# Half of the last memory layer moved into attention, a PSUM piece of its own for the rotation, and TensorE products without a reader

## The chip, the core and the metric

The kernel runs on one core of a Trainium2 chip. It is one launch; the metric is the time of that launch on the device in microseconds (us). The core has TensorE (matrix products, "PE" in the profile; its weight loads are "PEld"), VectorE ("DVE"), ScalarE ("ACT"), GpSimd ("POOL") and SyncE ("SP", which issues most DMAs). Each takes its own instructions in the order in which they were put. Products are written to PSUM, which has 8 banks of 2 KB in each of 128 partitions; everything else lies in SBUF.

## What is computed

A two-block network on an input `x` of 2 sequences ("batches") of 512 tokens and 512 features, all in float32. Block 0 is a state space layer with a quantised feed-forward layer before and after it. Block 1 is attention with a memory layer before and after it. Only block 1 matters here:

- The memory layer normalises `x` to `h` (mean and variance of a token), and adds half of `h` to `x`. From `h` it forms `q = h Wq` (64 features) and `Wr q` (48). Routing scores against 128 slots pick the best 8 slots of a token; a softmax over these of `q`'s scores against the keys weighs the slots' values. A gate of the token multiplies the result before it is added to `x`. The gate is made of `log1p(var(h))`, divided by its mean over all tokens of both batches, and of a small network `gelu(h Wu1 + bu1) Wu2`.
- Attention normalises `x`, makes 32 query heads and 8 key and value heads of 16 features, rotates queries and keys by position, applies a causal softmax, and adds the output product to `x`.

## The kernel before

**Tokens and tiles.** `x` is held in SBUF as eight tiles `x[t]` of 128 tokens by 512; tiles 0 to 3 are batch 0 and 4 to 7 are batch 1. A norm (`norm_parts`) has the steps `stats(t)` (L168, L169), `root` (square root on ScalarE, L172), `over` (reciprocal), `centre(t)` (L179) and `turn(t)`: four transposes on TensorE into a PSUM tile (L201) and a copy on ScalarE to the transposed `hT[b]` (L205).

**The last stages** are `memory(0)`, `attention` and `memory(1)`, one after the other. Each has its own PSUM pools. A pool has a tag and a number of buffers; a buffer is as large as the largest tile of the tag, and a new tile in a buffer waits until everything that read the old one is done. In the memory layers there are the tags `tr`, `mm`, `dd` and `y`, with two banks each. In attention there are `pq` (two buffers of two banks), `mx` (two of one bank), `av` (one) and `s` (one). `ps` puts a tile with a tag that attention hasn't got into `s`.

**Order.** Inside `in_order` the instructions of each engine stay in the order of the code. Outside, the planner of the framework orders them, and two ordered parts may be interleaved by it. The parts of `memory` behind the norm are ordered by the planner; the norm of `memory(1)` (`norm_in_order`) and all of attention are in order.

**Attention's start** (`attend`, first loop). For batch 0 it goes over five weight tiles `u` (keys, then four of queries), spread over iterations `n`. `qk` makes the projection in two halves of two products (L1425), then `hi` on ScalarE and `lo` and `r` on VectorE (L1414, L1415, L1438), which all read the projection. `rotate` of the tile before multiplies `hi` and `lo` by a permutation (L1448), into the second half of the same PSUM tile `p` that holds this iteration's projection; VectorE and GpSimd finish the rotation (L1451, L1452). `rotated` splits it again (L1463, L1464) and `spread_out` writes queries and keys as their products need them (L1474 to L1481). Between them lie the transposes of the norm's batch 1 (`turn`), the value product (L1488), and the first `maxima`.

**Attention's tiles.** 2 batches times 8 tiles of four heads, with four steps `j` each (64 steps). In step `j`:

- `maxima` for the next tile: scores on TensorE into `mx` (L1507), row maxima on VectorE (L1517);
- `weights_of`: mask and score products into both `pq` buffers (L1540, L1553), then the exponentials on ScalarE (L1559);
- `weigh` of the step before: products with the values into `av` (L1569);
- at j=0 `normalise` of the tile before: transposes into `s` (L1582), reciprocal and product on VectorE (L1589, L1590);
- `jobs`: a table of further pieces for step (tile, j), run after the above;
- after j=3 `turn_maxima`: transposes into `s` (L1527) and a copy on VectorE (L1529).

The order within a step is written out by hand:

```python
order = {
    0: (units[0], "weigh", "weights", "normalise", units[1]),
    1: ("weights", units[2], "weigh", units[3]),
    2: ("weights", units[4], "weigh", units[5]),
    3: ("weights", "weigh"),
}
```

In tiles 0 to 9 the jobs are batch 1's `qk` (halves in j=1 and j=2 of even tiles), `rotate` (j=3), `rotated` and `spread_out` (next, odd tile), and its values. In tiles 9 to 12 they are the output product of batch 0, one token tile in each: `out_turn` at j=1 (L1601, copy L1605) and `out_product` at j=2 (L1613, added to `x` at L1615). In tiles 14 and 15 they are three quarters of batch 1's output product. Nearly all of these use `s`.

**`memory(1)`** takes both batches: norm, first product `pz` (L1125) with a gelu, `pq` (L1151), `prq` (L1158), scores `psc` (L1167, L1168) with the choice of slots on VectorE (L1176 to L1192), exponential (L1195), transposes `pw` (L1198), the gate, the slots' product `pmo` (L1239) and its addition to `x` (L1242). `store` then writes `x` out in eight DMAs.

Of the kernel before, what the change touches and what calls it, by code (L numbers as in the profile page):

```python
# [10 lines left out]
F32 = mybir.dt.float32  # L11
# [63 lines left out]
        return (g, b) if g < NG else None  # L75


class Kernel:
    def __init__(self, tc, ctx, a, out):
        self.tc, self.nc, self.a, self.out = tc, tc.nc, a, out  # L80
        nc = self.nc
        self.const = ctx.enter_context(tc.tile_pool(name="const", bufs=1))
        self.xpool = ctx.enter_context(tc.tile_pool(name="xpool", bufs=1))
        self.dram = ctx.enter_context(
            tc.tile_pool(name="scratch", bufs=1, space=bass.MemoryType.DRAM)
        )
        masks = self.const.tile([P, 4, P], F32, name="masks")
        nc.sync.dma_start(out=masks, in_=a["masks"])
        self.ident = masks[:, 0, :]
        self.upper = masks[:, 1, :]  # L90
        self.below = masks[:, 2, :]
        self.ones = masks[:, 3, :]
        self.eps = self.const.tile([P, 2], F32, name="eps")
        nc.vector.memset(self.eps[:, 0:1], EPS)
        nc.vector.memset(self.eps[:, 1:2], 4.0 * EPS)
        self.npool = ctx.enter_context(tc.tile_pool(name="npool", bufs=1))
        self.x = [
            self.xpool.tile([P, D], F32, name=f"x{t}", tag=f"x{t}") for t in range(NT)
        ]
        self.normed = None  # L100
        self.load(0)

    def load(self, b):
# [48 lines left out]
        return t  # L152


    def norm_parts(self, tag, each=None, gain=None):

        nc, pool = self.nc, self.npool
        mv = pool.tile([P, NT, 2], F32, tag="mv", name=f"mv_{tag}", bufs=2)
        rstd = pool.tile([P, NT], F32, tag="rstd", name=f"rstd_{tag}", bufs=2)
        hT = [  # L160
            self.xpool.tile([P, KD, S], F32, tag=f"hT{b}", name=f"hT{b}_{tag}")
            for b in range(NB)
        ]
        done = {}

        def stats(t):
            st = pool.tile([P, 6], F32, tag="bnst", name=f"bnst_{tag}{t}", bufs=3)
            nc.vector.bn_stats(out=st, in_=self.x[t])  # L168
            nc.vector.bn_aggr(out=mv[:, t, :], in_=st)  # L169

        def root(t, to):
            nc.scalar.activation(  # L172
                rstd[:, t:to], mv[:, t:to, 1], AF.Sqrt, bias=self.eps[:, 0:1]
            )

        def centre(t):
            r = rstd[:, t : t + 1]
            h = pool.tile([P, D], F32, tag="h", name=f"h_{tag}{t}", bufs=3)
            nc.vector.tensor_scalar(  # L179
                out=h, in0=self.x[t], scalar1=mv[:, t, 0:1], scalar2=r,  # L180
                op0=ALU.subtract, op1=ALU.mult,
            )
            done[t] = h if each is None else each(t, h)

        def start(t):
            stats(t)
            root(t, t + 1)
            r = rstd[:, t : t + 1]
            nc.vector.reciprocal(r, r)
            centre(t)  # L190

        def over(t, to):
            nc.vector.reciprocal(rstd[:, t:to], rstd[:, t:to])

        self.norm_steps = stats, root, over, centre

        def turn(t, bank="tr"):
            h = done.pop(t)
            pt = self.ps(bank, [P, KD, P], f"hps_{tag}{t}")
            for k in range(KD):  # L200
                nc.tensor.transpose(pt[:, k, :], h[:, k * P : (k + 1) * P], self.ident)  # L201
            c = t % NC
            dst = hT[t // NC][:, :, c * P : (c + 1) * P]
            if gain is None:
                nc.scalar.copy(dst, pt)  # L205
            else:
                nc.vector.tensor_tensor(
                    out=dst, in0=pt, in1=gain.unsqueeze(2).to_broadcast([P, KD, P]), op=ALU.mult
                )

        return hT, start, turn

    def norm(self, tag, each=None, gain=None):
        hT, start, turn = self.norm_parts(tag, each, gain)
        for t in range(NT):
            start(t)
            turn(t)
        return hT

    def norm_in_order(self, tag, each):  # L220

        with self.in_order():
            hT, _, turn = self.norm_parts(tag, each)
            stats, root, over, centre = self.norm_steps
            for b in range(NB):
                for t in range(b * NC, (b + 1) * NC):
                    stats(t)
                root(b * NC, (b + 1) * NC)
            for b in range(NB):
                over(b * NC, (b + 1) * NC)  # L230
                for t in range(b * NC, (b + 1) * NC):
                    centre(t)
                    turn(t)
        return hT


# [810 lines left out]


    def memory_setup(self, pool):
        nc, a = self.nc, self.a  # L1050
        m = self.m = {}
        for name, shape in (
            ("m_wq", [P, KD, BOT]), ("m_wr", [BOT, RDIM]), ("m_keys", [BOT, NSLOT]),
            ("m_vals", [P, KD, NSLOT]), ("m_wvd", [P, KD, VB]), ("m_wvu", [VB, D]),
            ("m_wu1", [P, KD, P]), ("m_cols", [P, 2]),
        ):
            m[name] = pool.tile(shape, F32, name=name)
            nc.sync.dma_start(out=m[name], in_=a[name])
        m["rel"] = pool.tile([P, NSLOT], F32, name="m_rel")
        nc.sync.dma_start(out=m["rel"], in_=a["m_rel"].partition_broadcast(P))  # L1060
# [11 lines left out]
        for k in range(KD):  # L1072
# [1 line left out]
                p[:VB, :NSLOT], lhsT=m["m_wvd"][:, k, :], rhs=m["m_vals"][:, k, :],  # L1074
                start=k == 0, stop=k == KD - 1,
            )
        vd = pool.tile([VB, NSLOT], F32, name="m_vd")
        nc.scalar.copy(vd, p[:VB, :NSLOT])
        p = self.ps("tr", [P, D], "p_vu")
        nc.tensor.matmul(p, lhsT=vd, rhs=m["m_wvu"], start=True, stop=True)  # L1080
# [3 lines left out]
    def memory(self, n, then=None):  # L1084
# [3 lines left out]
        with self.tc.tile_pool(name=f"mem{n}", bufs=1) as pool:  # L1088
# [8 lines left out]
                )  # L1097
                return h

            hT = (self.norm_in_order if n else self.norm)(f"m{n}", each)  # L1100


            lv = pool.tile([P, NT], F32, name=f"lv{n}")
# [128 lines left out]
            with self.in_order():  # L1232
# [3 lines left out]
                for t in range(NT):  # L1236
# [13 lines left out]
                        root(t + 1 - NC, t + 1)  # L1250
                    if t == NC:
                        over(0, NC)
                        for one in range(NC):
                            if one == NC - 1:
                                turn(0)
                            centre(one)
                        for one in range(1, NC):
                            turn(one)
                if then is not None:
                    over(NC, NT)  # L1260
                    for t in range(NC, NT - 1):
                        centre(t)
                    return hT, turn, centre

# [47 lines left out]
    def attend(self, turn, centre):  # L1314
# [7 lines left out]
        def measure(n=1):  # L1322
            for one in ahead[:n]:
                self.maxima(0, 0, *one)
            del ahead[:n]


        for n in range(len(first) + 2):
            if n > 1:
                self.rotated(*first[n - 2])  # L1330
            p = self.ps("pq", [P, 2, S], f"pqk_{n}") if n <= len(first) else None
            for half in range(2):
                if n < len(first):
                    self.qk(*first[n], half, p[:, 0, :])
                if n > 3:
                    measure()
                if n < NC and not half:
                    turn(NC + n, "mx")
            if n == 0:
                centre(NT - 1)  # L1340
            if n == 1:
                self.project_values(0)
            if 0 < n <= len(first):
                self.rotate(*first[n - 1], p[:, 1, :])
            if n > 1:
                b, u = first[n - 2]
                tags = ("mx", "mx", "av", "s") if u == 4 else ("av", "s")
                for i, tag in enumerate(tags):
                    self.spread_out(b, u, i, tag)
# [9 lines left out]
        for t, u in ((0, 4), (2, 0), (4, 1), (6, 2), (8, 3)):  # L1359
# [4 lines left out]
            for i in range(4 if u == 4 else 2):  # L1364
                n, j = divmod(4 * t + 5 + i, 4)
                job(n, j, self.spread_out, 1, u, i, "s")
        job(3, 3, self.project_values, 1)
        for c in range(NC):
            job(9 + c, 1, self.out_turn, 0, c, 0, KD)
            job(9 + c, 2, self.out_product, 0, c, 0, KD, "s")  # L1370
            for j, f, *tag in ((1, self.out_turn), (2, self.out_product, "mx")):
                n, j = divmod(4 * 14 + j + c, 4)
                job(n, j, f, 1, c, 0, KD - 1, *tag)
# [9 lines left out]
        for n, (b, t, j) in enumerate(steps):  # L1383
            to = tiles[n // NC + 1] if n // NC + 1 < len(tiles) else None
            for one in order[j]:
                if one == "weights":
                    self.weights_of(b, t, j)
                elif one == "weigh":
                    if n:
# [19 lines left out]
        self.nc.scalar.copy(oT, pt)  # L1409
        for c in range(NC):  # L1410
            self.out_product(1, c, k, KD, "mx", {k: oT[:, c, :]})

    def parts(self, hi, lo, x):
        self.nc.scalar.copy(hi, x)  # L1414
# [207 lines left out]
def body(tc, a, out):  # L1622
    with ExitStack() as ctx:
# [8 lines left out]
        with k.banks("psum_e", dd=2, y=2, tr=2, mm=2):  # L1632
# [1 line left out]
            ctx.enter_context(k.weights("b", 6, 4))  # L1634
            k.attention_setup(ctx.enter_context(tc.tile_pool(name="attn_const", bufs=1)))
            parts = k.memory(0, lambda: k.norm_parts("a"))
        with k.banks("psum_b", pq=2, mx=2, av=1, s=1):
            k.attention(*parts)
        with k.banks("psum_c", **four):
            k.memory(1)  # L1640
        k.store()


# [137 lines left out]
```

## Time and profile before

| what | us |
|---|---|
| median of three runs | 2813.09 |
| lowest and highest of them | 2789.83, 2822.13 |
| the profiled execution, time | 2795.29 |
| its span | 2793.5 |
| TensorE busy in it | 2689.8 (96%) |
| VectorE busy | 2030.9 (73%) |
| ScalarE busy | 1102.6 (39%) |
| first step of attention's tiles | 2454 |
| last output product of attention added to `x` | 2720.9 |
| last product of `memory(1)` added to `x` | 2790.5 |

Times in the trace are us from the start of the span. A group row names the line, the engine, the operation, its output and inputs, and the shape. Two numbers in front of a timeline row are start and length; a bracket at its end is the idle time of the engine before it and what ended it. In a list of waits, the three numbers are total us, number of times and longest. In a table of stretches, the clock is the share of full speed that TensorE was granted. Matmul records overlap their successors, so the distance of starts tells their cost better than their length.

### The profile page before, as it was taken

What the parts mean: (1) busy time and instruction counts of PE and PEld (TensorE: products, weight loads), DVE (VectorE), ACT (ScalarE), POOL (GpSimd) and SP (SyncE); (2) the same over time, 40 slices, a digit from 0 to 9 for tenths busy, and PEclk for the clock granted to TensorE, in tenths of its full rate; (3) what the DMA queues carried; (4) which work ended last, traced back from release to release, by engine and by line L of the source; (5) the groups of instructions that cost most, each with busy time, mean ns of one, the idle gap of its engine ahead of it and who ended that gap; (6) DMA issues with size and microseconds to landing.
All of it is one profiled execution on the core that took longest, in us unless ns stands there. A gap on an engine that the chain in (4) does not pass through costs nothing.

```text
span 2793.5 us, 33412 instructions
## 1 busy us (share of the span) xinstructions
PE 2689.8 (96%) x12208; PEld 1398.5 (50%) x12208; DVE 2030.9 (73%) x3632; ACT 1102.6 (39%) x2411; POOL 522.1 (19%) x344
## 2 busy tenths in 40 slices
PE   8999999999999999999999999999999999788887
PEld 4444555555555555555555555555554444444443
DVE  7836877877888788787888878878886533555545
ACT  2214443544444344344443444434443212244442
POOL 0001131313313123132321322313230000110000
PEclk9999999999999999999999999999999999889996
DMA  7623133223223322322322332232121020000000
GB/s 209 198 89 113 72 107 128 87 91 123 96 83 124 113 72 103 129 87 80 126 105 83 121 105 80 106 128 87 68 99 46 27 84 1 0 1 1 1 1 31
DMA packets 75621, 237.77 MB, mean 85 GB/s; under 512 B 9825, under 2 KB 10401, under 8 KB 58945
## 3 DMA queue, kind: packets, MB, share of 16 engines
q1 hardware_dynamic: 70416, 226.00, 23.2%
q10 hardware_dynamic: 4752, 8.65, 0.8%
q8 instruction: 97, 1.59, 0.2%
q0 software_dynamic: 288, 0.98, 0.1%
q14 instruction: 68, 0.55, 0.1%
HBM read 223.80 MB, written 11.80 MB: 84 GB/s over the span
## 4 chain that ended last, share of the span: by engine, by line
PE 85%; DVE 9%; ACT 4%; issue 1%; DMA 0%; ACTq 0%; SPq 0%; DVEq 0%
PE pg L715 15%; PE po L832 14%; PE cp_h L715 14%; PE fo L501 5%; PE fmm L334 5%; PE py L989 4%; PE st L908 3%; PE fy L334 2%; DVE acc_h L729 2%; PE py L998 2%; PE cp_BT L715 2%; PE cp_CT L715 2%; PE ht L1042 2%; PE w L1553 1%; PE pqk L1425 1%; PE fdd L334 1%
## 5 line engine op out<-in xcount | busy, mean ns | idle before, releaser
L715 PE MATMUL pg<-hT_s,wi 128*128 128x512 f32 x1024 | 472.5, 604 | 14.4 <-issue 6.9
L832 PE MATMUL po<-wo,yg 128*128 128x512 f32 x1024 | 460.7, 593 | 0.5 <-DVE yg L1009 0.5
L715 PE MATMUL cp_h<-hT_s,wi 128*128 128x512 f32 x1024 | 460.6, 592 | 0.0
L806 DVE TENSOR_TENSOR_SCAN M<-rows,later 128x512 f32<-128x512 f32 x256 | 457.8, 1827 | 0.0
L1016 POOL TENSOR_TENSOR ssum<-ssum,sq 128x512 f32<-128x512 f32 x112 | 142.2, 1270 | 1233.0 <-ACT sq L1015 1233.0
L715 PEld LDWEIGHTS pg<-hT_s,wi 128*128 128x128 f32 x1024 | 184.2, 189 | 221.6 <-issue 213.4
L729 DVE SCALAR_TENSOR_TENSOR acc_h<-cp_h,small,acc_h 128x511 f32<-128x511 f32 (+2 forms) x384 | 286.1, 745 | 9.0
L832 PEld LDWEIGHTS po<-wo,yg 128*128 128x128 f32 x1024 | 184.8, 190 | 184.4 <-issue 183.6
L715 PEld LDWEIGHTS cp_h<-hT_s,wi 128*128 128x128 f32 x1024 | 184.6, 190 | 183.6 <-issue 183.6
L822 POOL TENSOR_TENSOR Cs<-CT,rows 128x768 f32<-128x768 f32 x128 | 251.9, 1968 | 17.6 <-PE py L998 15.7
L918 DVE SCALAR_TENSOR_TENSOR st<-st,whole,st 128x64 f32<-128x64 f32 x512 | 108.8, 274 | 125.7 <-ACT st L913 125.7
L734 ACT ACTIVATE th_h<-acc_h 128x512 f32<-128x512 f32 x128 | 80.5, 629 | 292.2 <-DVE acc_h L729 286.5
L861 ACT ACTIVATE hd<-ht,end 128x64 f32<-128x64 f32 x768 | 170.4, 323 | 35.8 <-DVE hc L853 35.7
L1015 ACT ACTIVATE sq<-yg 128x512 f32<-128x512 f32 x112 | 70.6, 630 | 286.9 <-DVE yg L1009 286.9
L820 DVE TENSOR_TENSOR M<-M,CB 128x512 f32<-128x512 f32 x256 | 164.4, 683 | 0.1
L811 ACT ACTIVATE M<-M 128x512 f32<-128x512 f32 x128 | 80.7, 630 | 199.1 <-DVE M L806 199.1
L853 DVE TENSOR_TENSOR hc<-ht,dt 128x512 f32<-128x512 f32 x128 | 88.0, 688 | 86.2 <-PE ht L1042 86.2
L1517 DVE CUSTOM_DVE_ANT_0 j<-s,future 128x384 f32<-128x384 f32 (+3 forms) x256 | 112.8, 486 | 48.8 <-PE s L1507 48.6
L989 PEld LDWEIGHTS py<-M,hc 128*64 128x64 f32 x2048 | 109.4, 136 | 68.2 <-issue 64.7
L989 PE MATMUL py<-M,hc 128*64 128x128 f32 x2048 | 140.5, 279 | 1.1 <-DVE M L820 1.1
L908 PEld LDWEIGHTS st<-hd,Btok 128*128 128x128 f32 x768 | 104.0, 191 | 70.0 <-issue 42.4
L738 DVE SCALAR_TENSOR_TENSOR v<-v,pg 128x512 f32<-128x512 f32 x128 | 87.4, 683 | 49.8 <-ACT v L849 47.7
(325 smaller groups left out, 3776.6 us busy)
## 6 DMA issues: line engine op xcount, KB each, us to landing
rows<-rows SPq DMA_DIRECT2D x128, 1024.0 KB, 4.7
wi<-in_w_in_dram SPq DMA_DIRECT2D x144, 256.0 KB, 3.5
wo<-in_w_out_dram SPq DMA_DIRECT2D x64, 256.0 KB, 3.1
keep<-w ACTq DMA_DIRECT2D x33, 256.0 KB, 3.5
wk<-keep SPq DMA_DIRECT2D x33, 256.0 KB, 2.7
wi<-in_q_dram SPq DMA_DIRECT2D x44, 128.0 KB, 3.1
sc<-in_s_dram SPq DMA_DIRECT2D x44, 128.0 KB, 3.2
wi<-in_q_dram SPq DMA_DIRECT2D x11, 256.0 KB, 3.3
```

Of the source, the lines that this page charges most:

```text
L334: nc.tensor.matmul(dst, lhsT=w[:, k, :], rhs=x[:, k, :], start=start and k == 0, stop=stop and k == 1, skip_group_check=True,)
L501: nc.tensor.matmul(po, lhsT=act[ht][:, b, c * P : (c + 1) * P], rhs=w2[ht], start=ht == 0, stop=ht == NHT - 1,)
L715: self.nc.tensor.matmul(p, lhsT=wt[:, k, :], rhs=self.hT[b][:, k, :], start=k == 0, stop=k == KD - 1)
L729: self.nc.vector.scalar_tensor_tensor(out=acc[:, s:], in0=p[:, : S - s], scalar=w[:, 3 - s : 4 - s], in1=acc[:, s:], op0=ALU.mult, op1=ALU ...
L806: self.nc.vector.tensor_tensor_scan(out=m, data0=rows[:, i, 0, :], data1=self.later, initial=0.0, op0=ALU.add, op1=ALU.mult,)
L820: self.nc.vector.tensor_tensor(out=m, in0=m, in1=sh["CB"], op=ALU.mult)
L822: self.nc.gpsimd.tensor_tensor(out=cur.Cs, in0=sh["CT"][:, P:].unsqueeze(1).to_broadcast([P, 2, S - P]), in1=cur.rows[:, :, 1, P:], op=ALU ...
L832: self.nc.tensor.matmul(self.po[c], lhsT=p2.yg[:, c * P : (c + 1) * P], rhs=self.wo[p2.ct], start=p2.q == 0, stop=p2.q == PAIRS - 1,)
L861: nc.scalar.mul(hd[:, c, ch], p1.pt[:, c, ch], self.dec["dt_end"][:, b * NC + c, h0 + i : h0 + i + 1],)
L908: nc.tensor.matmul(pst[:, c, :], lhsT=self.sh[p1.g, p1.b]["Btok"][:, c, :], rhs=hd[:, c, :], start=True, stop=True,)
L989: nc.tensor.matmul(py[ch, cs], lhsT=hc[:, c, ch], rhs=p1.M[i].rearrange("p (c t) -> p c t", c=NC)[:, c, :], start=c == 0, stop=c == 0, ski ...
L1016: nc.gpsimd.tensor_tensor(out=self.ssum, in0=self.ssum, in1=sq, op=ALU.add)
```

## The change

It has four parts.

1. **Memory in parts.** A class `Memory` holds the last memory layer cut into steps for one batch or one token tile: `learn`, `gelu`, `query`, `route`, `learned`, `score`, `weight`, `gate`, `add`. Batch 0's steps up to `weight` become jobs in attention's tiles 11 to 15; its norm's statistics stand behind the output products, which are moved closer together (tiles 9 to 11). All of their PSUM tiles go to `s`, since attention has no `tr`, `dd`, `y` of its own. `end_last`, after attention, does batch 1 and the gates and additions of both batches. The variance of `h` is now worked out from that of `x` (`spread`), and the second `bn_stats` and `bn_aggr` of each tile are gone from this layer. `memory(0)` keeps the old code. `norm_in_order` is gone.
2. **The rotation's piece.** In attention's start the projection and the rotation get a PSUM tile each, of the same tag `pq`, and `turn` comes after the second half of `qk`.
3. **Products that nothing reads.** `keep_up(n)` puts `n` products of bfloat16 constants, 128x128 by 128x512, into a tile that has no reader: two after each of the six `maxima` in attention's start (`s`), one in front of `weights_of` in every step but j=2 (`s`, 48 in all), six in front of the transposes of the norm that leads to attention (`dd`), and eight, then two, in front of the transposes of the last norm (`y`).
4. **Pools.** Three constants of the memory layer and an intermediate one lie in a pool that is closed after their use, whose space goes to the next pools; the last memory layer's small tiles lie in a pool that is open through attention.

```diff
@@ class Memory (new; steps shortened)
+    def half(self, t, h):
+        x = self.k.x[t]
+        self.nc.vector.scalar_tensor_tensor(
+            out=x, in0=h, scalar=0.5, in1=x, op0=ALU.mult, op1=ALU.add
+        )
+        return h
...
+    def learn(self, b):
+        pz = self.k.ps("dd", [P, S], f"pmz{n}_{b}")
+        for k in range(KD):
+            nc.tensor.matmul(
+                pz, lhsT=m["m_wu1"][:, k, :], rhs=self.hT[b][:, k, :],
+                start=k == 0, stop=k == KD - 1,
+            )
+        z, th = self.work("acc", f"mz{n}_{b}"), self.work("th", f"mt{n}_{b}")
+        nc.scalar.activation(z, pz, AF.Identity, bias=m["m_cols"][:, 0:1])
...
+    def weight(self, b, c):
+        if c == 0:
+            self.wT[b] = self.work("wT", f"mw{n}_{b}")
+        pw = self.k.ps("dd", [P, P], f"pmw{n}_{b}_{c}")
+        nc.tensor.transpose(pw, self.at.pop(b * NC + c), self.k.ident)
+        nc.scalar.copy(self.wT[b][:, c * P : (c + 1) * P], pw)
@@ memory_setup
+        with self.tc.tile_pool(name="mem_made", bufs=1) as made:
+            self.memory_constants(pool, made)
...
+            at = made if name in ("m_vals", "m_wvd", "m_wvu") else pool
+            m[name] = at.tile(shape, F32, name=name)
@@ memory(0), before the norm that leads to attention
                         over(0, NC)
+                        self.keep_up(6, "dd")
@@ end_last (new)
+            for t in range(NC, NT):
+                stats(t)
+            root(NC, NT)
+            over(NC, NT)
+            for t in range(NC, NT):
+                centre(t)
+                self.keep_up(2 if t > NC else 8, "y")
+                m.turn(t)
+        m.spread()
+        m.learn(1)
+        m.gelu(1)
+        m.query(1)
+        m.route(1)
+        m.learned(1)
+        m.gate(0)
+        for c in range(NC):
+            m.score(1, c)
+            m.weight(1, c)
+        for t in range(NC):
+            m.add(t)
+        m.gate(1)
+        for t in range(NC, NT):
+            m.add(t)
@@ attend, start
                 self.maxima(0, 0, *one)
+                self.keep_up(2)
...
-            p = self.ps("pq", [P, 2, S], f"pqk_{n}") if n <= len(first) else None
+            p = self.ps("pq", [P, S], f"pqk_{n}") if n < len(first) else None
+            rot = self.ps("pq", [P, S], f"prot_{n}") if 0 < n <= len(first) else None
             for half in range(2):
                 if n < len(first):
-                    self.qk(*first[n], half, p[:, 0, :])
+                    self.qk(*first[n], half, p)
...
-                if n < NC and not half:
+                if n < NC and half:
                     turn(NC + n, "mx")
...
-                self.rotate(*first[n - 1], p[:, 1, :])
+                self.rotate(*first[n - 1], rot)
@@ attend, jobs: at(n, f) is step n of 64, tile n // 4, j = n % 4
         for c in range(NC):
-            job(9 + c, 1, self.out_turn, 0, c, 0, KD)
-            job(9 + c, 2, self.out_product, 0, c, 0, KD, "s")
+            at(37 + 2 * c, self.out_turn, 0, c, 0, KD)
+            at(38 + 2 * c, self.out_product, 0, c, 0, KD, "s")
+            at(38 + 2 * c, stats, c)
+            at(46 + c, centre, c)
+            at(47 + c, m.turn, c)
+            at(56 + 2 * c - (c == 3), m.score, 0, c)
+            at(57 + 2 * c - (c == 3), m.weight, 0, c)
+        at(45, root, 0, NC)
+        jobs[divmod(46, NC)].insert(0, (over, (0, NC)))
+        for n, f in ((51, m.learn), (52, m.query), (53, m.gelu), (54, m.route), (55, m.learned)):
+            at(n, f, 0)
@@ attend, steps
                 if one == "weights":
+                    if j != 2:
+                        self.keep_up(1)
                     self.weights_of(b, t, j)
@@ keep_up (new)
+    def keep_up(self, n, tag="s"):
+        p = self.ps(tag, [P, NC, P], f"up{self.ups}")
+        self.ups += 1
+        for _ in range(n):
+            self.nc.tensor.matmul(
+                p, lhsT=self.mask[:, 0, :],
+                rhs=self.mask[:, 1:2, :].to_broadcast([P, NC, P]), start=True, stop=True,
+            )
```

## The prediction

> **What bounds the kernel now.** I read first the page's slices (where TensorE, "PE", is not full), then busy time by stage, then the chain of waits of each stage, then the timeline of single steps.
>
> The page's slices, of 70 us each:
> ```profile
> PE   8999999999999999999999999999999999788887
> ...
> PEclk9999999999999999999999999999999999889996
> ```
> TensorE is full up to slice 34; only the last six, which are the memory layer, attention and the second memory layer, are not, and only there does its clock drop. The change touches these alone. Busy time by stage (length, then PE, PEld, DVE, ACT, POOL, clock, DMA share, GB/s):
> ```profile
> 2393.00:2460.00 67.00, 52.62 (x203) 30.16 (x205) 31.75 (x81) 20.70 (x35) 12.67 (x10) 0.81 0.00 1
> 2460.00:2660.00 200.00, 178.90 (x1629) 95.92 (x1628) 119.91 (x470) 87.20 (x138) 12.78 (x10) 1.00 0.01 1
> 2660.00:2716.00 56.00, 49.23 (x427) 26.01 (x427) 23.08 (x84) 22.91 (x38) 0.00 (x0) 0.97 0.00 1
> 2716.00:2794.00 78.00, 59.92 (x150) 26.62 (x149) 46.21 (x139) 20.46 (x42) 0.00 (x0) 0.71 0.07 27
> ```
> Attention's 16 tiles (2454 to 2716) run at 89% PE and full clock: work added there costs nearly its own length. The tail after 2716 is a latency chain at a clock of 0.71: work taken from there is cheap to take. What TensorE waited for, first within 2407 to 2454 (attention's start), then within 2454 to 2716 (us, times, longest):
> ```profile
> PE pqk L1448 <- DVE r L1438: 5.7, 3, 2.1
> ...
> PE w L1540 <- ACT w L1559: 11.2, 25, 0.7
> PE prot L1448 <- DVE r L1438: 4.1, 5, 0.8
> PE pm L1527 <- DVE r L1451: 3.9, 5, 0.8
> PE av L1569 <- ACT w L1559: 1.5, 1, 1.5
> ...
> PE pao L1613 <- ACT q L1477: 0.7, 1, 0.7
> ```
> The steady wait is for the exponentials (11.2). All `prot`, `pm` and `pao` rows are waits for the one-bank PSUM tag "s": its reader has to finish first. The fillers in the steps use that same tag. One even tile shows what this means:
> ```profile
> 2466.66 1.98 PE L1425 MATMUL pqk<-hT_a,a_wqk 128*128 128x512 f32 x4
> 2468.48 0.39 PE L1540 MATMUL w<-mask 128*128 128x128 bf16 x4
> ...
> 2470.73 0.47 PE L1448 MATMUL prot<-hi,spread 128*128 128x512 f32 x1 [0.81 <-DVE r L1438]
> ```
> The bank is not free until 2470.7, 2.3 us after the projection; today TensorE does 1.4 us of `weights_of` and `weigh` in that time.
>
> **The tail.** Last `x` at 2720.87, end 2793.5: 72.6 us for both halves. After it only batch 1 is left:
> - norm: statistics to 2722.5, root and reciprocal 0.7, then four times centre 0.55 and add 0.66 (the second statistics, 0.69 + 0.18 a tile, go) = 4.8, last transpose and copy 1.2: to 2729;
> - `learn` and `query`, 8 products at 0.86 = 6.9; q copy 0.58, `route` 1.0, rq copy 0.58: to 2738; gelu beside it. Ln (table load 1.28) is beside too;
> - four scores of 2.05 on DVE (8 instructions at 0.28) = 8.2, batch 0's four adds at 0.75 = 3, gates about 2: to 2751;
> - exponential, transpose, copy, gate 2; four adds 3 to 5; last store 3.0 as now: to 2760.
>
> Gain 33. With the clock at half throughout, 8 us more (25); with everything hidden, 37. `keep_up(8)` and its pairs lie where TensorE waited 6.4 for `h_m` in all: free.
>
> **Attention's start.** `rotate` shares a tile with the projection, so it waits for `r` of the next one: 5.7 in three waits. With its own piece it waits only for its inputs. The projection's pieces now follow each other in one slot, whose readers need 2.1 (hi 0.58, lo 0.69, r 0.68 and hand-overs); turn 0.43, rotate 0.7 and spread 0.9 cover 2.0 of that: gain about 5.5. The 12 fillers of `measure` cost at most 12 x 0.23 (the nearest row, a one-pass 128x512 product of L1474, starts each 0.23 at full clock) = 2.8, of which 1.3 falls into waits for `top`; and they bear on the half clock from 2440 to 2461, worth up to 3 to 4. `turn` behind the second half of `qk` moves a copy behind `hi`: 0. I take -7 (ends -3 and -9). `keep_up(6)` in front of `turn` lies in a 2.5 wait for `h_a`: 0, and up to -3 if the clock is back sooner; I take -1. The constants' pool that is closed early makes `a_wv` and the first weights wait for `p_vu` (2343.6): with them, on SP's queue, `rope`, `future` and `a_wo` behind. 3.6 MB take some 16 us at the 159 to 362 GB/s at which they came (2266 to 2288); first use is 2401: 0.
>
> **Fillers in the tiles.** 48, three a tile. Those of j=1 fall mostly into the 0.8 wait for the exponentials, once `normalise` has been read (bank free 1.6 after its start, before that wait ends): 0 in most tiles. Those of j=0 stand behind `turn_maxima`, whose reader the step needs anyway: 0.23. Those of j=3: 0.23 plus the bank. 32 x 0.23 = 7.4, with five visible ones of j=1 1.2. The bank's waits, behind which `weights_of`, and so ScalarE's exponentials and the next `weigh`, are queued:
> - even tiles 0 to 8, behind `qk`: 2.3 instead of 0.81, 1.4 x 5 = 7;
> - odd tiles to 7, behind `spread_out`: 0.7 (the `pao <- ACT q` row) x 4 = 2.8; tile 2 at j=1, where the copy queues behind the exponentials, 1.4;
> - tiles 9 and 10, j=3, behind `out_product`: product end to DVE's `x` read 0.95 x 2; tiles 12, 13 and 15 behind copies, 0.7 + 0.7 + 0.3: 3.6. Of j=1, tiles 10 to 14 have such a wait in place of the 0.8 for the exponentials: 1.5 over it.
>
> Sum 25. Its lower end is 8 (no wait beyond the fillers), its upper 33.
>
> Here a rule matters. The Trainium skill, "TensorE: Matmul & The Clock Gate", section "Part 1: The HAM clock gate", lets the clock fall only after an idle window of some 3.4 us. By it, waits of up to 2.3 cost no clock and fillers in the steps buy none. But the row of the one 1.5 wait says otherwise:
> ```profile
> 2664.00:2668.00 4.00, 2.54 (x22) 1.37 (x24) 2.11 (x7) 2.82 (x5) 0.00 (x0) 0.80 0.00 0
> 2668.00:2672.00 4.00, 3.37 (x30) 1.99 (x30) 1.76 (x5) 1.94 (x2) 0.00 (x0) 0.78 0.00 0
> ```
> 0.20 x 4 + 0.22 x 4 = 1.7 of clock lost, about 3.4 us at half. By the row each long wait may cost 1.5 more, by the rule 0. Since the 2.1 waits of 2424 to 2432 left the clock at 1.00, I take the rule for the forecast and the row for a rival.
>
> **Memory's first half in attention.** On PE: transposes 4 x 0.6, `learn` and `query` 6.9, `route` 0.9, `learned` 1.0, scores 4 x 0.72, weights 4 x 0.33: 15.3. All use "s", so: `turn_maxima` behind a copy in tiles 9 to 13, 4 x 0.68 + 0.4 = 3.1; jobs at j=0 behind `normalise`, 5 x 0.45 = 2.2; in tiles 14 and 15 `out_turn` behind scores and weights, 2.5. 23 together (ends 15 and 30). DVE gets 15 us over five tiles (scores 8.2, centres 4.8, gelu 2.5) at 58% busy: hidden, but `maxima` behind gelu waits 1. ACT's copies: 8 us at 43%, in the waits above. Statistics and root stand within attention already (`bnst_m` at 2663.3, root at 2664.3); an earlier root has its inputs sooner: the 1.5 wait for the exponentials and half its clock loss go, -2.5. Moved `out_turn` and `out_product` are the same work.
>
> Sum: 25 + 23 + 1 - 2.5 = 46 in the tiles, -33 in the tail, -8 at the start: +5. The profiled run took 2795.3 (span 2793.5), so 2800; the median of the three runs is 2813 (2790 to 2822), 18 above that run, so about 2817. I predict 2816. About 1% (28 us) is the least that these runs tell from no change.
>
> **Rivals.**
> - *Fillers hide* (0.22): the bank is free in time or ScalarE sets the pace anyway. Tiles 8 + 17 - 2.5, tail -36, start -9: -22, 2791. For it: 11.2 of waits for exponentials. Against: `prot` and `pao` rows show the bank's wait in the open.
> - *The clock falls in the steps* (0.20), the slower side: the waits for "s" let TensorE cool as the 1.5 wait did. Some 16 waits of over 0.7, at 1.5 each, +24: +29, 2842. It decides if the clock from 2454 to 2720 is under about 0.87. For it the two rows above; against it 2460 to 2660 at 1.00 with ten 0.8 waits.
> - *The tail doesn't shorten as it should* (0.13): the two batches overlap there today (batch 1's products lie between batch 0's scores), so that taking one away leaves batch 1's chain at half clock. Gain 20: +18, 2831.
> - *Forecast* (0.45): 2800 to 2830.
>
> **How the numbers follow.** Faster by over 1% needs the first rival nearly whole, with the prologue's best: 0.13. Slower by over 1% is half of the second, a fifth of the third and a little of the forecast's edge: 0.16. The rest is 0.71. The range, 2784 to 2842, runs from the first rival with the tail's best to the second, and takes in the runs' spread.
>
> **What would show it.** After: tail from last `x` to the end 37 to 42 with a clock above 0.8; `prot` without waits before its tiles and the first exponential 6 earlier; attention's tiles some 46 longer, with waits at the filler for `r` of L1438 (five of about 2.2), `q`, `x` and copies. Wrong if the filler's rows show no waits (then faster), if the clock in the tiles drops (slower), or if a scheduler outside the written order spreads the tail's products.

## The result and the profile after

| | before | after |
|---|---|---|
| median of 22 runs each, us | 2808.2 | 2822.3 |
| lowest to highest, us | 2788.8 to 2822.1 | 2809.2 to 2836.1 |
| profiled execution, time (span), us | 2795.3 (2793.5) | 2829.5 (2827.7) |

The ratio after to before is 1.0063, with a 95% interval of 1.0046 to 1.0080: 18 us slower by the ratio (the two medians lie 14 apart), within the 1% that was taken as "no change". The forecast was +5. The spans of the two profiled runs differ by 34.2: before's lies 13 below its median, after's 7 above. The stages below are therefore read for where time went, and the ratios for how much.

The page's slices of after, 71 us each:
```profile
PE   8999999999999999999999999999999998889887
...
PEclk9999999999999999999999999999999997998988
```
The last slices show a shorter tail at a higher clock than before, and the slices with attention's tiles (34 to 36) are no longer full, with a clock that drops to 0.7 in one of them. Stretches of after, with the same columns as before (length, PE, PEld, DVE, ACT, POOL, clock, DMA share, GB/s), cut where stages begin: tiles 0 to 8, tiles 9 to 14, tile 15 up to the last output product, the tail.
```profile
2449.69:2623.88 174.19, 149.91 (x1193) 77.64 (x1193) 85.82 (x330) 62.86 (x99) 10.18 (x8) 0.87 0.00 1
2623.88:2760.38 136.50, 118.95 (x864) 61.36 (x864) 68.77 (x254) 49.48 (x82) 2.54 (x2) 0.89 0.00 1
2760.38:2789.20 28.82, 25.29 (x168) 12.39 (x168) 11.34 (x32) 10.02 (x19) 0.00 (x0) 1.00 0.00 1
2789.20:2827.70 38.50, 27.75 (x84) 11.82 (x82) 24.66 (x81) 11.53 (x27) 0.00 (x0) 0.79 0.15 55
```
The same cut of before's trace, of which tiles 0 to 8, tiles 9 to 14 and the tail are shown, gives the balance (us, and the granted clock behind the @):
```profile
2452.10:2598.70 146.60, 128.97 (x1167) 69.28 (x1167) 85.41 (x330) 62.86 (x99) 10.22 (x8) 0.97 0.01 1
2598.70:2697.80 99.10, 90.12 (x793) 48.57 (x793) 57.45 (x224) 43.00 (x67) 2.56 (x2) 0.98 0.00 1
...
2720.90:2793.50 72.60, 55.98 (x142) 25.57 (x142) 42.30 (x132) 19.43 (x41) 0.00 (x0) 0.69 0.08 29
```

| stage | before | after | difference |
|---|---|---|---|
| up to `p_vd`, among the memory layers' constants | 2341.0 | 2343.4 | +2.4 |
| from there to the first tile (`memory(0)` from there on, attention's start) | 111.1 @0.83 | 106.3 @0.84 | -4.8 |
| tiles 0 to 8 | 146.6 @0.97 | 174.2 @0.87 | +27.6 |
| tiles 9 to 14 | 99.1 @0.98 | 136.5 @0.89 | +37.4 |
| tile 15 to the last output product | 23.1 @1.00 | 28.8 @1.00 | +5.7 |
| tail | 72.6 @0.69 | 38.5 @0.79 | -34.1 |

Tiles 0 to 8 hold no memory work: of what the change brings, only the products without a reader ("fillers") lie there. What TensorE waited for in after's tiles (us, times, longest):
```profile
PE up L1658 <- DVE r L1688: 10.0, 5, 2.0
PE pm L1777 <- DVE r L1701: 3.9, 5, 0.8
PE up L1658 <- DVE x L1865: 3.1, 4, 0.8
PE w L1790 <- ACT w L1809: 2.2, 7, 0.6
...
PE up L1658 <- ACT q L1727: 2.0, 3, 0.7
```
`up` is the filler. Five times it waits 2.0 for the last reader of the projection, and 0.7 or 0.8 behind other readers of the one-bank tag "s". The wait for the exponentials (`w`, 11.2 before) has shrunk to 2.2: the fillers stand where it was, and take more than it gave. The start's wait of 5.7 for `r` is gone; one of 0.2 is left:
```profile
PE pqk L1675 <- DVE r L1688: 0.2, 1, 0.2
```

### The profile page after: what moved, and what is told of

It reads as the page before. It is cut to its first block, busy times and chain, and to the rows that moved or that the text cites. A ratio compares the mean times of both kernels' runs of the same rounds, so it can differ in the third digit from the quotient of the medians.

```text
span 2827.7 us, 33591 instructions
## 1 busy us (share of the span) xinstructions
PE 2720.9 (96%) x12288; PEld 1410.3 (50%) x12288; DVE 2031.1 (72%) x3627; ACT 1101.7 (39%) x2418; POOL 522.3 (18%) x344
## 4 chain that ended last, share of the span: by engine, by line
PE 85%; DVE 9%; ACT 4%; issue 1%; DMA 1%; POOL 0%; SPq 0%; ACTq 0%; DVEq 0%; POOLq 0%
PE pg L881 14%; PE po L998 14%; PE cp_h L881 13%; PE fo L667 5%; PE fmm L500 5%; PE py L1155 4%; PE st L1074 3%; PE fy L500 2%; DVE acc_h L895 2%; PE py L1164 2%; PE cp_CT L881 2%; PE cp_BT L881 2%; PE ht L1208 2%; PE w L1803 2%; PE av L1819 1%
## 5 line engine op out<-in xcount | busy, mean ns | idle before, releaser
L1809 ACT ACTIVATE w<-w 128x1024 f32<-128x1024 f32 (+3 forms) x128 | 83.1, 701 | 106.7 <-PE w L1803 104.9
```

## The experiments

Each ratio is to the kernel before on the same chip, with its 95% interval. Fillers have no reader, so a kernel without them leaves out nothing of the output. Each trace is of one execution, and not always a typical one: in experiments 2, 3 and 7 it is the fastest run of its kernel (of 6, 6 and 16), in experiment 11 the slowest of 12. A stage's clock in it shows what can happen; for what a kernel usually gets, the text gives the median, over its runs, of the granted clock of the whole run (0.978 to 0.982 in the sets of runs of before, 0.981 for after).

**1. After without the fillers in the tiles.**
```diff
-                    if j != 2:
-                        self.keep_up(1)
                     self.weights_of(b, t, j)
```


> The changed kernel without the 48 products in front of weights_of; those of attention's start and of the last norm stay. Theory (the fillers' bank costs): 7 us of products, 17 us of waits for s go, so some 25 us faster than the changed kernel, 2797, ratio to before 0.996; the rows 'up <- DVE r', 'up <- DVE x', 'up <- ACT q' are gone. Rival (the fillers hold the clock, and pay for their waits): no faster than the changed kernel, 1.005 or more, with a granted clock in the tiles well below the 0.86 of the changed kernel's profile. Second rival (the memory parts in the tiles cost it all): 1.004.

Measured: 0.9918 (0.9896 to 0.9939), median 2778.9, faster than both kernels. The 48 fillers cost 1.0063 - 0.9918 = 1.45%, 41 us, where the forecast had 25. The tiles of this kernel, 0 to 8 and 9 to 14:
```profile
2437.65:2588.57 150.92, 134.71 (x1166) 71.26 (x1166) 85.41 (x330) 62.88 (x99) 10.18 (x8) 0.93 0.00 1
2588.57:2712.40 123.83, 112.36 (x846) 58.60 (x846) 68.26 (x254) 49.40 (x82) 2.55 (x2) 0.90 0.00 1
```
Against after, tiles 0 to 8 are 23 shorter and tiles 9 to 15 are 15 shorter; the clock is 0.93 instead of 0.87 in the first and hardly higher (0.90 for 0.89) in tiles 9 to 14. The median clock of the runs is 0.988.

**2. The fillers in another bank.** The same 48 products are written to the `pq` buffer that the step's own products overwrite next, not to "s".
```diff
-                    if j != 2:
-                        self.keep_up(1)
                     self.weights_of(b, t, j)
...
         ps = [self.ps("pq", [P, 2, S], ...) for x in range(2)]
+        if j != 2:
+            nc.tensor.matmul(
+                ps[0][:, 0, :].rearrange("p (c t) -> p c t", c=NC), lhsT=self.mask[:, 0, :],
+                rhs=self.mask[:, 1:2, :].to_broadcast([P, NC, P]),
+                start=True, stop=True, skip_group_check=True,
+            )
```


> The changed kernel, but the 48 products write into the first pq bank of weights_of itself, in front of the mask products that begin it anew, instead of into s. Same products, no wait for a reader of s. Theory (the bank, not the product, costs): the 17 us of waits go and 7 to 11 us of products stay, 2805 to 2808, ratio 0.999 to 1.000, between the changed kernel and the one without tile fillers. Rival (clock): products without the waits are the best of all, clock in the tiles near 1.00, ratio under 0.996.

Measured: 0.9931 (0.9905 to 0.9958), faster than was expected. The products cost 0.13%, 4 us, over having none (the intervals overlap), where in "s" they cost 41. One even tile at j=3, first in after (TensorE alone; start, length):
```profile
2501.74 1.98 PE L1675 MATMUL pqk<-hT_a,a_wqk 128*128 128x512 f32 x4
2505.72 0.38 PE L1658 MATMUL up<-mask 128*128 128x512 bf16 x1 [2.00 <-DVE r L1688]
2505.93 0.38 PE L1790 MATMUL w<-mask 128*128 128x128 bf16 x4
```
and the same step with the filler in `pq`:
```profile
2479.34 1.98 PE L1673 MATMUL pqk<-hT_a,a_wqk 128*128 128x512 f32 x4
2481.16 0.38 PE L1788 MATMUL w<-mask 128*128 128x512 bf16 x1
2481.38 0.39 PE L1794 MATMUL w<-mask 128*128 128x128 bf16 x4
...
2483.42 0.47 PE L1696 MATMUL prot<-hi,spread 128*128 128x512 f32 x1 [0.59 <-DVE r L1686]
```
The filler itself holds TensorE for 0.21 to 0.22 in both (distance of starts). In "s" it stands 2.0 for the bank with the whole step behind it; in `pq` the step runs during that time, and only the rotation waits, 0.59. Tiles 0 to 8 of this kernel:
```profile
2435.62:2582.00 146.38, 131.67 (x1193) 70.60 (x1194) 85.24 (x330) 62.90 (x99) 10.19 (x8) 1.00 0.00 1
```
The clock is 1.00 here, but this is the fastest of six runs, and 146.4 is what before took without any (146.6). That the fillers hold the clock is not shown: the median clock of the runs is 0.988, the same as without them (experiment 1). The rival's number (under 0.996) came true; its reason, that these products are the best of all, did not.

**3. Before with the fillers in the tiles alone**, in "s" as in after (`keep_up` itself is added too).
```diff
+                    if j != 2:
+                        self.keep_up(1)
                     self.weights_of(b, t, j)
```


> The kernel before with nothing but the 48 products in front of weights_of, in s. Theory: 15 us in tiles 0 to 8 and some 6 us after them, 2829, ratio 1.008; five waits of 2.0 for r, several of 0.7 for q and x. Slower rival (these waits make TensorE cool): the clock in the tiles falls from 1.00 to under 0.90 and 10 to 24 us more go, ratio 1.011 to 1.016. If the fillers were harmless: 1.002.

Measured: 1.0100 (1.0080 to 1.0121), +28 us. The slowdown needs no other part of the change. Its tiles 0 to 8, and its first wait there:
```profile
2446.72:2619.60 172.88, 148.78 (x1193) 76.97 (x1193) 85.72 (x330) 62.91 (x99) 10.19 (x8) 0.89 0.00 1
```
```profile
PE up L1419 <- DVE r L1449: 10.0, 5, 2.0
```
They are 26.3 longer than before's. At full clock an even tile went from 17.5 to 19.3 (tile 2 to 20.2) and an odd one from 12.7 to 14.0, which makes 4 x 1.8 + 2.6 + 4 x 1.3 = 15; in these two executions the other 11 come with the clock, 0.89 instead of 0.97.

**4. No fillers anywhere.**
```diff
     def keep_up(self, n, tag="s"):
-        p = self.ps(tag, [P, NC, P], f"up{self.ups}")
-        self.ups += 1
+        return
```


> The changed kernel with keep_up doing nothing anywhere: no products without a reader, in the tiles, in attention's start or in the two norms. Theory: the tiles gain 25 us as without tile fillers; at the start and in the norms the products were free and worth up to 4 us of clock, so 2797 to 2801, ratio 0.996 to 0.998. Rival (the start's fillers keep the clock at 0.96 there): 6 to 9 us slower than without tile fillers alone, 1.000.

Measured: 0.9956 (0.9941 to 0.9971). Without fillers the change is a gain of 12 us. The fillers of the start and the norms, which only experiment 1 has on top of this, give 0.0038 (11 us, give or take 7) more, where the forecast had 1. The traces place only part of it: the tail takes 36.7 to 39.0 in the kernels with these fillers and 40.1 and 40.5 in the two that have the short tail without them. The median clock of the runs is 0.980, against 0.988 in experiment 1: these fillers do go with a higher clock.

**5. The rotation's piece alone, on before.**
```diff
-            p = self.ps("pq", [P, 2, S], f"pqk_{n}") if n <= len(first) else None
+            p = self.ps("pq", [P, S], f"pqk_{n}") if n < len(first) else None
+            rot = self.ps("pq", [P, S], f"prot_{n}") if 0 < n <= len(first) else None
...
-                if n < NC and not half:
+                if n < NC and half:
                     turn(NC + n, "mx")
...
```


> The kernel before with the rotation's own PSUM piece and turn behind the second half of qk, and nothing else. Theory by the forecast's step: the three waits of 5.7 us for r shrink to under 1, 5.5 us faster, ratio 0.998. By what the run without fillers showed (start of attention 98 us instead of 111): 10 us and more, because the half clock behind it goes too, 0.996. Rival (the waits only move): 1.000.

Measured: 0.9985 (0.9965 to 1.0006), -4 us with an interval that includes 0. In the trace the start is 12 shorter than before's (98.8 at a clock of 0.90 for 111.1 at 0.83), and tiles 9 to 14 are 9 longer (107.9 at a clock of 0.86 for 99.1 at 0.98), where nothing was changed: so much can two single executions differ. The wait for `r` at the start is 0.2, as in after.

**6. The memory parts alone**: after, with experiment 4's edit and experiment 5's taken back.
```diff
-            p = self.ps("pq", [P, S], f"pqk_{n}") if n < len(first) else None
-            rot = self.ps("pq", [P, S], f"prot_{n}") if 0 < n <= len(first) else None
+            p = self.ps("pq", [P, 2, S], f"pqk_{n}") if n <= len(first) else None
...
-        p = self.ps(tag, [P, NC, P], f"up{self.ups}")
-        self.ups += 1
+        return
```


> The changed kernel without any product without a reader and with the rotation as before: of the change only the memory parts (and pools). Theory: tail 33 shorter, tiles 23 to 29 longer at full clock, so 4 to 10 us faster than before, ratio 0.996 to 0.999; with a half clock in tiles 9 to 14 as in the run without fillers (0.85), 1.000. Rival (the parts cost as much as the tail gives): 1.002 or more.

Measured: 0.9972 (0.9952 to 0.9993), -8 us. The tail is 40.1, 32.5 shorter; tiles 9 to 15 are 29.3 longer (125.0 and 26.5 for 99.1 and 23.1). Tiles 0 to 8 stay at before's 146.5 and 0.97. The stretch with tiles 9 to 14:
```profile
2600.00:2725.00 125.00, 113.31 (x845) 59.38 (x845) 68.31 (x254) 49.40 (x82) 2.55 (x2) 0.89 0.00 1
```
The clock is 0.89 with no filler anywhere. The memory jobs' own waits may bring it down, but that is not shown: experiment 5 had 0.86 there without these jobs. Experiments 5 and 6 add up: -4 - 8 = -12, as in 4.

**7. Small products in place of the wide ones**, with the same waits.
```diff
-                        self.keep_up(1)
+                        self.keep_up(1, small=True)   # p[:, 0, :], rhs self.mask[:, 1, :]
```


> The changed kernel, but each of the 48 tile fillers is a 128x128 product instead of 128x512: a quarter of the work, the same place in the queue and the same wait for s. Theory (the waits cost, the products don't): 32 x 0.17 = 5 us faster than the changed kernel at most, 2813 to 2818, ratio 1.003 to 1.005; the five waits of 2.0 for r stay. Rival (it is the products): as without tile fillers, 0.992. Third (big products keep the clock up, small ones don't): slower than the changed kernel, 1.010.

Measured: 1.0105 (1.0079 to 1.0131). A quarter of the products' work gains nothing, and the interval (22 to 37 us slower than before) lies above the first expectation; it is the third that came true, by which small products hold the clock less (1.010). `up <- DVE r` is again 10.0 in five waits, so the waits are the same, and the median clock of the runs is 0.9725, against 0.981 in after.

**8. Four products for one**, which wait once and keep TensorE at work longer.
```diff
-                        self.keep_up(1)
+                        self.keep_up(4)
```


> The changed kernel with four products of 128x512 at each of the 48 places instead of one, after the same waits. If products bring no clock: three more of 0.23 at 33 places in the open, 23 us, and up to 8 at j=1, so 23 to 31 us slower than the changed kernel, ratio 1.014 to 1.017, clock in the tiles under 0.92 as there. Rival (enough products keep TensorE warm behind the waits): clock in tiles 0 to 14 at 0.97 or more, which gives some 25 us back, ratio 1.005 to 1.008.

Measured: 1.0138 (1.0102 to 1.0174). Tiles 0 to 8:
```profile
2449.00:2628.00 179.00, 155.72 (x1274) 80.71 (x1272) 85.20 (x330) 62.45 (x99) 10.20 (x8) 0.96 0.00 1
```
With three more fillers at each place and the same five waits of 2.0, the clock here is 0.96 instead of 0.87, close to what the rival named, and the median of the runs is 0.987. So after the same waits the clock rises with the work of the filler: 0.9725, 0.981 and 0.987 in experiment 7, in after and here. But the products cost more than the clock returns: 21 us slower than after.

**9. No filler at j=3.**
```diff
-                    if j != 2:
+                    if j < 2:
```


> The changed kernel with tile fillers at j=0 and j=1 only. Theory: the waits at j=3 (five of 2.0 behind qk, four of 0.7, two of 0.8 behind out_product and the rest) and 16 products go: 7 + 2.8 + 3.6 + 3.7 = 17 us and the clock that falls with them, 10 more, so 2795 to 2805, ratio 0.996 to 0.999. Rival (all fillers cost alike): a third of the 41 us, 2809, 1.001. The five waits of 2.0 are then gone and the clock of tiles 0 to 8 above 0.95.

Measured: 0.9970 (0.9951 to 0.9989), 26 us faster than after (1.0063 - 0.9970). Sixteen of the 48 fillers carry most of the cost; in the trace tiles 0 to 8 are back at 150.6 and 0.97.

**10. The filler of j=3 behind `weigh`**: same number, same bank, later in the step.
```diff
-                    if j != 2:
+                    if j < 2:
                         self.keep_up(1)
                     self.weights_of(b, t, j)
...
+                    if j == 3:                        # after weigh
+                        self.keep_up(1)
```


> The changed kernel with the filler of j=3 behind weigh instead of in front of weights_of: the same 48 products, in the same bank s, but weights_of and weigh are no longer queued behind the bank's reader. Theory (what is queued behind the wait costs): even tiles wait 0.8 for r as before, in the filler instead of in rotate; odd ones not at all. The same as without fillers at j=3 plus 16 x 0.23 = 4 us, 2801, ratio 0.998. Rival (a filler in s costs wherever it stands): as the changed kernel, 1.006.

Measured: 1.0006 (0.9979 to 1.0033), 16 us faster than after. The wait for the projection's reader is now 0.7:
```profile
PE up L1660 <- DVE r L1690: 3.6, 5, 0.7
```
A place a few instructions later in the queue, with the step's work in front of it, gives back 1.3 of each 2.0.

**11. No filler at j=3 behind `qk`** (even tiles 0 to 8), which takes away the five waits of 2.0 and leaves the others.
```diff
-                    if j != 2:
+                    if j != 2 and not (j == 3 and n < 36 and n // NC % 2 == 0):
```


> The changed kernel without the five fillers at j=3 of the even tiles 0 to 8, those that wait 2.0 for r behind qk; the other 43 stay. Theory by waits at full clock: 5 x 1.8 = 9 us faster than the changed kernel, 2811, ratio 1.003. If these five waits are what lets the clock fall in tiles 0 to 8 (0.87 to 0.89 with them, 0.93 to 1.00 without), some 10 to 15 us more: 2798 to 2803, ratio 0.998 to 1.000, and the clock of tiles 0 to 8 at 0.95 or more. If the many waits of 0.7 take it as well, the clock there stays at 0.90 or less and the ratio at 1.003.

Measured: 1.0035 (1.0015 to 1.0055), 8 us faster than after (give or take 7): an even tile at full clock takes 17.8 here for 19.3 with the filler (experiment 3), which makes 5 x 1.5 = 7.5, and no more is seen. Tiles 0 to 8:
```profile
2444.00:2614.00 170.00, 151.97 (x1189) 79.22 (x1188) 85.91 (x330) 62.65 (x99) 10.34 (x9) 0.85 0.00 1
```
The clock is 0.85 in this execution, the slowest of 12, though no wait of TensorE in these tiles is longer than 0.8. The long waits are not needed for the half clock. Nor does the sum of the listed waits decide it: it is 18.6 here and 18.1 in before's tiles 0 to 8, which ran at 0.97.

**12. Without the fillers in the tiles, the memory jobs of j=3 (tiles 9 to 14) behind the next tile's first `weigh`.** It asks whether the jobs' own waits can be covered as in experiment 10.
```diff
-                    if j != 2:
-                        self.keep_up(1)
...
+                    if j == 0 and n // NC > 9:        # behind weigh
+                        for f, args in jobs.get((n // NC - 1, 3), ()):
+                            f(*args)
...
-            for f, args in jobs.get((n // NC, j), ()):
-                f(*args)
+            if j == 3 and 9 <= n // NC < 15:
+                pass
+            else:
+                for f, args in jobs.get((n // NC, j), ()):
+                    f(*args)
```


> Without tile fillers, and the jobs of j=3 in tiles 9 to 14 (out_turn, turn, learn, learned, weight) run in the next tile's j=0 behind weigh, so that turn_maxima no longer waits for their readers. Theory (the memory parts cost their products and these waits): five waits of 0.67 and one of 0.35 go, 3.7 us, and a window of half clock less in tiles 9 to 14, 5: 2770 to 2775, ratio 0.989 to 0.990. Rival (the waits only move to normalise, which needs s too): as without tile fillers, 0.992.

Measured: 0.9931 (0.9909 to 0.9953), no gain over experiment 1 (0.9918). Tiles 9 to 14 are 5 shorter in the trace (118.9 at 0.87) and tile 15, which now holds a job of tile 14, is 4 longer (30.3). The `pm` waits for these jobs' copies (3.8 in experiment 1) are gone and one of 1.5 for the gelu has come; that this gained nothing may lie in the clock, whose median is 0.985 for 0.988, but is not shown.

## Why the prediction was right and where it was not

The predicted 2816 lies 6 below the median measured, and its direction and its "no change" hold. That it came so near is partly luck: the forecast counted from 2811, 3 above before's median, and two terms were off in opposite directions. The sum by its parts, in us by the ratios:

| part | predicted | measured |
|---|---|---|
| memory parts, tiles and tail | -33 + 21.5 = -11.5 | -8 (exp. 6) |
| rotation's piece | -5.5 | -4 (exp. 5) |
| fillers of the start and the norms | -1.5 - 1 = -2.5 | -11 (exp. 1 against 4) |
| fillers in the tiles | +25 | +41 (after against exp. 1); +28 on before (exp. 3) |
| whole | +5 | +18 |

In the two traces attention's tiles are 71 longer where 46 were forecast, but these two executions differ by 34 where the ratio says 18.

**The tail** was right: -33 predicted, -34.1 in after and -32.5 in experiment 6. Its clock was 0.79, a little under the 0.8 that was named. The rival by which it would not shorten is out.

**Memory in attention** was 21.5 and measured 29.3 in its tiles. Work and single waits were counted at full clock; the clock there went from 0.98 to 0.89. At 125 us this is at most 125 x 0.11 - 99 x 0.02 = 12 us, enough for the 8 that are missing. But no run holds the clock fixed, and these same tiles differed by 9 between before and experiment 5 with nothing changed in them. By the ratio the memory parts gave 8 for the 11.5 that were forecast.

**The start.** Step and cause hold: the wait of 5.7 for `r` is gone. The profiles show more than was forecast (-12), the ratio less (-4, give or take 6), so a gain clear of noise is not shown.

**The fillers in the tiles** are the step that was off. The mechanism was right and is in the open: a wait for "s" at the filler, with `weights_of` and ScalarE's exponentials queued behind it. Its places and readers were right too (`r`, `q`, `x`, copies), and 2.0 was measured for the predicted 2.3. The clean part was sized well: for tiles 0 to 8 the prediction's even and odd waits and products come to about 15, as the full-clock tiles of experiment 3 show. The missing term is the clock, which was put at nothing. The forecast weighed the Trainium skill, "TensorE: Matmul & The Clock Gate", "Part 1: The HAM clock gate", against the row of one 1.5 wait, and took the rule: no cost for waits under 3.4. In these traces the rule does not hold, as the row said: tiles 0 to 8 ran at 0.87 with no wait over 2.0, and at 0.85 with none over 0.8 (experiment 11). The prediction's own sign of being wrong, a clock that drops in the tiles, is what was seen. The same page, in "A second HAM failure mode: psum-queue depth-cycling", tells of a clock that goes back and forth when TensorE idles briefly between groups; that describes this case better, and the prediction did not weigh it.

How much went with the clock can be estimated from all runs. In each kernel time follows the run's mean clock, by 19 to 23 us for each 0.01 (14 in experiment 3, whose clocks span only 0.004). With 21 us for 0.01, the kernels that differ in their tile fillers alone come to:

| kernel | median us | median clock | estimate at 0.981, us |
|---|---|---|---|
| after | 2822 | 0.981 | 2822 |
| without tile fillers (1) | 2779 | 0.988 | 2794 |
| in `pq` (2) | 2784 | 0.988 | 2799 |
| small products (7) | 2831 | 0.9725 | 2813 |
| four for one (8) | 2839 | 0.987 | 2852 |

So of the 43 us between the medians of after and experiment 1, about 28 remain at equal clock, near the 25 of the forecast, and 15 go with the clock. After's set of runs may have had a lower clock by chance (before took 2808 beside it and 2798 to 2803 in the other sets; 5 us are worth some 0.003), so the clock's share is some 8 to 15.

The rival "the clock falls in the steps" named this with its point of decision at 0.87 for all tiles; there it was 0.89 in after's trace, between the forecast and this rival. It charged 24 for about 16 long waits. What is seen beyond the 25 that were forecast at full clock is 41 - 25 = 16 on the whole kernel, and beyond the measured clean length 11 in tiles 0 to 8 of experiment 3; and a price per long wait is not what was seen, since taking out five of the longest gave back 8, about their length. "Fillers hide" is out: the bank's wait was in the open in every run that had it.

**The fillers of the start and the norms** were worth more than was forecast, by the ratios. The prediction gave them up to 4 us of clock at the start and 1 in front of the norm; the median clock is 0.008 higher with them, worth some 17 us by the estimate above, before what the products themselves cost. About 3 of the 11 are in the tail; in which stage the rest lies is open. The start's profiles do not show it: 95.8 to 106.6 with these fillers, 98.4 and 98.8 with the rotation's piece but without them.

Open stays which waits put TensorE to half clock. Why the fillers in the tiles cost 41 on after but 28 on before is open in part: in experiment 3 the median clock fell only from 0.979 to 0.9765, worth 5 us, where after lost 8 to 15.

## What to carry to other kernels

A product that nothing reads is not free because TensorE would wait anyway: if its bank has one buffer it waits for the last reader, and everything queued behind it waits too (41 us for 48 products here, against 4 in a bank that is free at that moment). Ask first when its bank is free, then where it stands in the queue, and only then what it buys in clock. More filler work did hold more clock here, but in the full tiles it never paid for its length; at the start and in the norms it did (11 us, give or take 7). When a rule says that short waits cost no clock, look for a row of the trace that says otherwise before a term is put at nothing.

## What was not expected of the hardware

**The same wait costs clock in one place and none in another.** After has a wait of 2.00 for `r` at 2503.7 to 2505.7 and again at 2541.5 to 2543.5. The first of these stretches holds the first wait, the other three the second and what follows:
```profile
2504.00:2508.00 4.00, 2.29 (x27) 1.17 (x26) 1.29 (x2) 1.00 (x3) 0.00 (x0) 1.00 0.01 4
2540.00:2544.00 4.00, 2.00 (x9) 0.78 (x7) 2.12 (x8) 0.58 (x1) 0.00 (x0) 1.00 0.01 2
2544.00:2548.00 4.00, 3.21 (x29) 1.66 (x26) 0.69 (x1) 0.66 (x2) 0.98 (x1) 0.66 0.00 0
2548.00:2552.00 4.00, 4.00 (x29) 1.93 (x29) 2.00 (x5) 0.58 (x1) 0.28 (x1) 0.50 0.00 0
```
The clock stays at 1.00 after the first and is at half for 4 x 0.68 + 4 = 6.7 us after the second, although TensorE's products fill that time but for one wait of 0.8: up to 3.4 lost.

**It is not the same from run to run.** Nine kernels have the same instructions in the stage from `p_vd` to the first tile (after, and experiments 1, 2 and 7 to 12). It took 95.8 three times at a clock of 0.96, 101.3 to 101.5 three times at 0.88, and 106.2 to 106.6 three times at 0.83 or 0.84: steps of about 5 us, with nothing between. Over after's 22 runs, time and mean granted clock go together with a correlation of -0.99, 22 us for each 0.01 of clock (2836.1 at 0.974, 2809.2 at 0.986). A difference of 10 us between two single profiles of such a kernel says nothing by itself; many runs of each do.
